# A third tile for the weighted values of a graph attention, in room taken from a buffer that is used only at the end

## The chip, the cores and the metric

The kernel runs on one core of a Trainium2 chip, as one launch. The metric is the device time of that core in microseconds (us), from the first instruction to the last. Six parts of the core appear below: PE (TensorE, the matrix multiplications, with PEld for its weight loads), DVE (VectorE), ACT (ScalarE), POOL (GpSimd, which here issues the gathers), SP (SyncE, which issues the other loads and stores), and the DMA engines that carry out the transfers.

## The reference

A layer of a graph network on 6250 nodes of 128 features and 200000 edges, which come sorted by their target node `dst`. Two convolutions over the edges come first, then the attention with 8 heads of 16 channels, which the change is about:

```
h = relu(layernorm(x))
h = mesh_conv(h, ...);  h = silu(group_norm(h)) + (silu(t_emb) @ tm_w + tm_b)
h = mesh_conv(h, ...);  h = silu(group_norm(h)) + h_in
q, k, v = (h @ qw + qb), (h @ kw + kb), (h @ vw + vb)      # n x 8 x 16 each
logits = (q[dst] * k[src]).sum(-1) * scale + (edge_attr @ ew + eb)
amax   = segment_max(logits, dst)
pe     = exp(logits - amax[dst])
ssum   = segment_sum(pe, dst)
w      = pe / clip(ssum[dst], 1e-06)
o      = segment_sum(w * v[src], dst)
out    = x + h + group_norm(o @ ow + ob)
```

All of it is in float32.

## The kernel before

The 200000 edges are cut into 196 chunks (`NCH`) of 1024 edges, that is 8 tiles (`TPC`) of 128 edges, one edge in each of the 128 partitions. The first convolution, the second and the attention each go through all chunks, one after the other; `pipeline` (L1011) writes the program of such a stage, and the class `Stage` of the attention gives it the steps. Each engine works through its instructions in the order in which the program issues them, and waits on semaphores for the others.

In step n of the attention the program issues, roughly in this order:

- `fetch` for chunk n + 2. SP loads the query table's rows (`pk`), the edges' relative targets (`rel`) and edge attributes; POOL issues eight indirect gathers (L314), each of which brings the key and value rows of 128 edges into one of eleven tiles `g`, `ge`, `gl`. The first gather of a chunk is held until PE's last product `qe` of an earlier chunk is through.
- `second` for a chunk s, which lies about a run of chunks behind: the one-hot `oh` of the edges' targets (L945 on DVE; for the last 40 chunks, `BY_ACT`, L1828 and L1829 on ACT), then `add_late`, which adds an earlier chunk's sums to the running sums (L1776, L1780, L1782 on DVE), then `sums` (L1757): 8 matmuls on PE, one for each tile (the trace counts each as two), of `oh` with the tile `v`, into one of two PSUM tiles `us0` and `us1` that take turns.
- `values_ahead` for the next chunk, s + 1: `weighted` (L1750 on DVE) writes the products of the gathered values with the weights `pe` into its tile `v`.
- `merge` for the chunk before, s - 1: L1790, L1793, L1764, L1766, L1767, L1768 on DVE compare its maxima, which `sums` left in `us`, with the running ones; L1770 and L1772 on ACT take two exponentials.
- `logits` for chunk n (L1687, L1692, L1695 on DVE, L1689 on ACT), `compared` (L940, L941 on ACT) and the products `qe` (L1672 on PE) for the next chunk.
- `early`: `columns` for the chunk after s + 1. ACT copies three groups of columns into that chunk's tile `v` (L1746, L1942, L1943).

The segment maxima are taken for runs of up to G = 8 chunks at once, by scans on DVE (L1722, L1725) between transposes on PE (L1718, L1729). The scans read segment marks, `nbs` and `nbe`, which `load_runs` (L1697) loads. The chunks are handled from the last edge to the first; `k.j` is NCH - 1 less the chunk's number, so it counts down to 0. Whenever a block of nodes has all its edges, its finishing (reciprocal of the sum L1266, output product L1105 and L1126, norm L1281 and below) is put between the steps.

The last seven steps (`ENDS`) follow an order written out by hand, the string `ENDING`; `ending` goes through its words, each a letter for the step and a number for the chunk's `j`. Its words n5, n3 and n1 load segment marks, in turn into the pool `bp` and into the pool `bq`.

A tile `v` holds 8 x 145 float32 values in each partition, 4640 bytes. It comes from a pool with two buffers:

```
k.v = vp.tile([P, TPC, VK + H + 1], FP, name="v", bufs=2)
```

so the columns of a chunk may be written once the sums of the chunk two before it have been read out. The pool `bq` is opened when the third chunk has been completed (`EARLY` = 3), at the point where the memory of a larger tile of the lead-in comes free:

```
if k.c == EARLY - 1:
    kept.ohs.close()
    gs[-1] = pool("gl", 1, side="right").tile([P, TPC, KV], FP, name="gl")
    self.bq = pool("bq", 1, side="right")
```

It holds one pair of marks, 2 x 2048 bytes in each partition. `lh_i` (L136) is a tile of indices of 784 bytes in each partition among the constants, and is used in the first convolution alone.

Of the kernel before, what the change touches and what calls it, by code (L numbers as in the profile page):

```python
# [11 lines left out]
FP = mybir.dt.float32  # L12
BF = mybir.dt.bfloat16
I32 = mybir.dt.int32
# [11 lines left out]
P = 128  # L26
D = 128
H = 8
# [3 lines left out]
TPC = 8  # L32
# [21 lines left out]
ENDS = 7  # L54
# [5 lines left out]
VK = H * (HD + 1)  # L60
# [7 lines left out]
def kernel(ctx: ExitStack, tc: tile.TileContext, x, src, dst, eat, w, out):  # L68
# [12 lines left out]
    NCH = -(-EI // TPC)  # L81
# [6 lines left out]
    const = ctx.enter_context(tc.tile_pool(name="const", bufs=1))  # L88
# [8 lines left out]
    hpc = gpc.enter_context(tc.tile_pool(name="hpc", bufs=1))  # L97
    kept = SimpleNamespace(h0=hpc.tile([P, NW, D], FP, name="h0"))
# [34 lines left out]
    nc.vector.tensor_scalar(minus_p, iota_p, -1.0, None, ALU.mult)  # L133
    src_i = const.tile([P, EW], I32, name="src_i")
    not_first = const.tile([P, 1], FP, name="not_first")
    lh_i = const.tile([P, NCH], I32, name="lh_i")  # L136
    wab = {}

    def new_wab(pool, i):
# [194 lines left out]
    def last_product():  # L334
        return next((i.name for i in reversed(nc.cur_bb.bb.instructions) if i.engine == mybir.EngineType.PE), None)
# [233 lines left out]
    def steps_of(i):  # L569


        ends, due, n = {}, {}, 0
        for m in spread(i):
            ends[n + m] = list(range(n, n + m))
            due.setdefault(n + m + (i == 3 or n < NCH - SOON), []).extend(ends[n + m])
            n += m
        waiting, todo, left = [], [], NCH
        while left:
            n = len(todo)
            waiting += due.get(n, ())  # L580
            steps = min([m for m in due if m > n], default=n + 1) - n
            k = -(-len(waiting) // steps)
            todo.append(waiting[:k])
            waiting = waiting[k:]
            left -= k
        return ends, todo
# [351 lines left out]
    def compared(k):  # L938

        nc.scalar.activation(k.ohT[:WN, :], k.rel, AF.Square, bias=minus_p[:WN])  # L940
        nc.scalar.activation(k.ohT[:WN, :], k.ohT[:WN, :], AF.Relu, bias=1.0, scale=-4.0)  # L941
# [686 lines left out]
    def attention(general=False):  # L1628
        if general:
# [3 lines left out]
        pool = lambda n, b, **kw: es.enter_context(  # L1633
            tc.tile_pool(name=f"{n}a{general:d}", bufs=b, reuse_waits="tile", **kw))
# [6 lines left out]
        gp, wk, vp = pool("gp", 1), pool("wk", 2), pool("vp", 1)  # L1641
# [13 lines left out]
        def banks():  # L1655
            return ps_.tile([P, 2, 512], FP, name="blk", tag="blk")
# [40 lines left out]
        def load_runs(run, bp):  # L1697

            nb = {}
            for name, d_ in (("nbs", nbs_d), ("nbe", nbe_d)):  # L1700
                nb[name] = bp.tile([G * H, EPC], BF, name=name)
                nc.sync.dma_start(
                    out=nb[name][:len(run) * H, :],
                    in_=d_[NCH - 1 - run[-1]:NCH - run[0], :, :].rearrange("c h e -> (c h) e"))
            return nb
# [35 lines left out]
        def heads(k):  # L1741
            return k.v[:, :, :VK].rearrange("p t (h c) -> p t h c", c=HD + 1)

        def columns(k):
            k.v = vp.tile([P, TPC, VK + H + 1], FP, name="v", bufs=2)
            nc.scalar.copy(heads(k)[:, :k.nt, :, HD], k.pe)  # L1746

        def weighted(k):
            v4 = heads(k)
            nc.vector.tensor_tensor(  # L1750
                v4[:, :k.nt, :, :HD], k.g[:, :k.nt, D:].rearrange("p t (h c) -> p t h c", c=HD),
                k.pe[:, :, :, None].to_broadcast([P, k.nt, H, HD]), ALU.mult)

        def sums(k, wide):
            k.u = us[k.c % 2]
            for t in range(k.nt):
                nc.tensor.matmul(k.u[:, :wide], lhsT=k.oh[:, t, :], rhs=k.v[:, t, :wide],  # L1757
                                 start=(t == 0), stop=(t == k.nt - 1))
# [38 lines left out]
        def add_late(k):  # L1797
            if k.j < ONE:
                add(k, t3[:, 0:1, :], 1)
            else:  # L1800
                add(k, t3[:, bass.ds(k.win, 2), :], 2)
# [21 lines left out]
        def halves_by_act(k):  # L1823
            k.oh = pools["oh"].tile([P, TPC, P], FP, name="oh")
            for t in range(k.nt):
                if t == TPC // 2:
                    yield
                nc.scalar.activation(k.oh[:, t, :], iota_j, AF.Square, bias=k.dm[:, t:t + 1], scale=-1.0)  # L1828
            nc.scalar.activation(k.oh[:, :k.nt, :], k.oh[:, :k.nt, :], AF.Relu, bias=1.0, scale=-1.0)  # L1829

        def onehot_by_pool(k, behind):
            k.oh = pools["oh"].tile([P, TPC, P], FP, name="oh")
            for t in range(k.nt):
                follows(nc.gpsimd.tensor_scalar(
                    k.oh[:, t, :], iota_j, k.dm[:, t:t + 1], None, ALU.is_equal), behind)

        class Stage:
# [3 lines left out]
            lg, j, both = None, 0, None  # L1841
# [14 lines left out]
            def complete(self, k):  # L1856

                for a in range(0, TPC, 4):
                    more = banks()
                    m4 = more.rearrange("p a (t c) -> p (a t) c", c=KV)  # L1860
                    for t in range(4):
                        nc.tensor.matmul(m4[:, t, :], lhsT=k.ohS[:, (a + t) * P:(a + t + 1) * P], rhs=late,
                                         start=True, stop=True)
                    nc.vector.tensor_tensor(k.g[:, a:a + 4, :], k.g[:, a:a + 4, :], m4, ALU.add)
                if k.c == EARLY - 1:
                    kept.ohs.close()
                    gs[-1] = pool("gl", 1, side="right").tile([P, TPC, KV], FP, name="gl")
                    self.bq = pool("bq", 1, side="right")

            def products(self, k):  # L1870
                products(k, [(k.ohT[:KW], k.pk[:KW])])
# [94 lines left out]
            def ending(self, ks, marks):  # L1966

                every = {NCH - 1 - c: k for c, k in ks.items()}
                every.update({k.j: k for k in self.sums + self.late})
                runs = {NCH - 1 - run[0]: [NCH - 1 - c for c in run] for run in steps_of(3)[0].values()}  # L1970
                of = {j: r for r, js in runs.items() for j in js}
                firsts, low, hot, lgs = {}, {}, {}, {}
                nbs = {of[ENDS - 1]: self.nb}
                seen = {ENDS - 3: last_product()}
                self.residuals_of_last()
                for word in ENDING.split():
                    what, j = word[0], int(word[1:])
                    k = every.get(j)
                    if what == "f":
                        kept.seen = seen[j]  # L1980
                        every[j] = self.fetch(NCH - 1 - j)
                        kept.seen = None
                    elif what == "c":
                        compared(k)
                    elif what == "q":
                        self.products(k)
                        seen[j - 2] = last_product()
                    elif what == "l":
                        firsts[j] = self.firsts(k)
                        next(firsts[j])  # L1990
                        lgs[of[j]] = self.lg
                    elif what in "ra":
                        next(firsts[j], None)
                    elif what == "n":
                        nbs[j] = load_runs([NCH - 1 - i for i in runs[j]], self.bp if len(nbs) % 2 == 0 else self.bq)
                    elif what == "t":
                        low[j] = maxima([every[i] for i in runs[j]], lgs[j], nbs[j], self.bp, True)
                        next(low[j])
                        next(low[j])
                    elif what in "szw":  # L2000
                        next(low[j], None)
                    elif what == "d":
                        self.columns(k)
                    elif what == "v":
                        weighted(k)
                    elif what == "o":
                        hot[j] = halves_by_act(k)
                        next(hot[j])
                    elif what == "p" and j in hot:
                        next(hot[j], None)  # L2010
                    elif what == "p":
                        onehot_by_pool(k, kept.behind)
                    elif what == "u":
                        sums(k, VK + H + 1)
                    elif what == "m":
                        self.merge(k)
                    else:
                        add_late(k)
                self.sum_residuals()
# [144 lines left out]
```

## Time and profile before

| | |
|---|---|
| time, median of 3 runs | 7012.45 us |
| the three runs | 7008.08, 7012.45, 7033.32 us |
| the profiled execution | 6977.15 us, with a span of 6975.4 us |
| PE busy in the span | 3884.5 us (56%) |
| DVE busy | 4886.9 us (70%) |
| ACT busy | 3365.8 us (48%) |
| POOL busy | 4465.4 us (64%) |
| DMA, mean rate over the span | 92 GB/s |

The span is the time between the first and the last instruction of the one execution that the profiler recorded. A row of the profile names the line, the engine, the operation and the tiles that it writes and reads, then the shapes. In the groups the time after the bar is the busy time of the group, then the mean of one instruction in ns, then how long the engine was idle just before these instructions, with what ended the idle time: "issue" is time in which the engine waited for nothing that the profile shows, "remote" an event that could not be put down to one instruction. In rows by time the first number is the start, in us from the start of the span, the second the length, and in brackets stands the idle time before it.

The attention takes the stretch from about 4690 us to the end of the span.

### The profile page before, as it was taken

What the parts mean: (1) busy time and instruction counts of PE and PEld (TensorE: products, weight loads), DVE (VectorE), ACT (ScalarE), POOL (GpSimd) and SP (SyncE); (2) the same over time, 40 slices, a digit from 0 to 9 for tenths busy, and PEclk for the clock granted to TensorE, in tenths of its full rate; (3) what the DMA queues carried; (4) which work ended last, traced back from release to release, by engine and by line L of the source; (5) the groups of instructions that cost most, each with busy time, mean ns of one, the idle gap of its engine ahead of it and who ended that gap; (6) DMA issues with size and microseconds to landing.
All of it is one profiled execution on the core that took longest, in us unless ns stands there. A gap on an engine that the chain in (4) does not pass through costs nothing. (4 is left out here: it accounts for less than half of the span.)

```text
span 6975.4 us, 66960 instructions
## 1 busy us (share of the span) xinstructions
PE 3884.5 (56%) x20796; PEld 3580.4 (51%) x20797; DVE 4886.9 (70%) x6981; ACT 3365.8 (48%) x5296; POOL 4465.4 (64%) x4714
## 2 busy tenths in 40 slices
PE   5555554555555555555555555545555565555555
PEld 4555554554455555555555454544455555445554
DVE  6677777776767667676777777755666667667766
ACT  5555555555555555555555555532222223223465
POOL 4666666666666666666666666665666666666664
PEclk8666666777777666666677777766776767767677
DMA  4223323322232222222233333333444444444442
GB/s 123 75 73 83 102 74 85 80 75 79 77 81 76 65 71 68 70 71 67 69 88 88 84 89 85 88 99 99 119 120 115 119 118 125 120 122 115 118 119 81
DMA packets 384808, 640.95 MB, mean 92 GB/s; under 512 B 91440, under 2 KB 250652, under 8 KB 382827
## 3 DMA queue, kind: packets, MB, share of 16 engines
q0 software_dynamic: 175056, 410.03, 22.4%
q1 hardware_dynamic: 208170, 226.05, 11.5%
q8 instruction: 168, 2.75, 0.2%
q14 instruction: 198, 1.62, 0.1%
q10 hardware_dynamic: 1216, 0.49, 0.0%
HBM read 588.85 MB, written 48.48 MB: 91 GB/s over the span
## 5 line engine op out<-in xcount | busy, mean ns | idle before, releaser
L314 POOL DMA_INDIRECT g<-b_d,src_i x3078 | 2917.0, 948 | 1590.5 <-issue 861.5
L1431 PE MATMUL u<-h,oh 128*128 128x129 f32 (+1 forms) x6252 | 1363.5, 393 | 1573.9 <-issue 963.0
L1431 PEld LDWEIGHTS u<-h,oh 128*128 128x128 f32 x6252 | 1231.0, 294 | 1706.6 <-issue 1056.4
L314 POOL DMA_INDIRECT g<-kv_d,src_i x995 | 948.0, 953 | 552.6 <-issue 270.0
L1392 PE MATMUL m<-pk,ohT 101*128 101x128 f32 x6252 | 1054.2, 327 | 331.3 <-issue 315.5
L1392 PEld LDWEIGHTS m<-pk,ohT 101*128 101x128 f32 x6252 | 991.5, 243 | 355.6 <-issue 340.6
L1757 PE MATMUL us<-v,oh 128*128 128x145 f32 x3126 | 670.0, 374 | 527.3 <-issue 242.7
L1399 DVE TENSOR_TENSOR h<-m,g 128x1024 f32<-128x1024 f32 x392 | 474.3, 1210 | 695.1 <-remote 640.9
L1757 PEld LDWEIGHTS us<-v,oh 128*128 128x128 f32 x3126 | 591.7, 260 | 602.0 <-issue 370.4
L1672 PE MATMUL qe<-pk,ohT 101*128 101x136 f32 x3126 | 566.3, 351 | 264.2 <-ACT ebs L1689 193.1
L1423 ACT ACTIVATE h<-h 128x1024 f32<-128x1024 f32 (+2 forms) x394 | 413.0, 1048 | 568.5 <-issue 414.1
L1672 PEld LDWEIGHTS qe<-pk,ohT 101*128 101x128 f32 x3126 | 526.2, 252 | 302.8 <-ACT ebs L1689 217.7
L940 ACT ACTIVATE ohT<-rel,minus_p 96x1024 f32<-96x1024 bf16 x588 | 668.9, 1138 | 15.6 <-issue 11.3
L941 ACT ACTIVATE ohT<-ohT 96x1024 f32<-96x1024 f32 x588 | 619.9, 1054 | 18.8
L1403 DVE TENSOR_REDUCE var<-sq 128x64 f32<-128x1024 f32 x392 | 474.2, 1210 | 172.1 <-ACT sq L1401 78.8
L314 POOL DMA_INDIRECT ge<-kv_d,src_i x408 | 388.9, 953 | 230.5 <-issue 109.7
L945 DVE TENSOR_TENSOR oh<-cps,dm 128x1024 f32<-128x1024 f32 x392 | 474.3, 1210 | 75.3 <-remote 65.8
L1436 ACT ACTIVATE u<-u,mask 128x129 f32<-128x129 f32 (+1 forms) x688 | 230.6, 335 | 533.5 <-remote 480.6
L1421 DVE TENSOR_TENSOR h<-h,cps 128x1024 f32<-128x1024 f32 (+2 forms) x394 | 477.4, 1212 | 13.5
L1422 DVE TENSOR_TENSOR h<-h,cps 128x1024 f32<-128x1024 f32 (+2 forms) x394 | 477.4, 1212 | 13.5
L1418 DVE TENSOR_TENSOR h<-h,cps 128x1024 f32<-128x1024 f32 (+2 forms) x394 | 474.5, 1204 | 0.8
L1401 ACT ACTIVATE sq<-h 128x1024 f32<-128x1024 f32 x392 | 411.6, 1050 | 119.8 <-DVE h L1399 101.5
(332 smaller groups left out, 4399.4 us busy)
## 6 DMA issues: line engine op xcount, KB each, us to landing
rel<-rel_d SPq DMA_DIRECT2D x291, 384.0 KB
g<-b_d,src_i POOLq DMA_INDIRECT x3078
pk<-a_d SPq DMA_DIRECT2D x552, 46.0 KB
g<-kv_d,src_i POOLq DMA_INDIRECT x995
ohT<-in_eat_dram SPq DMA_DIRECT2D x291, 40.0 KB
ge<-kv_d,src_i POOLq DMA_INDIRECT x408
a_d<-n_o SPq DMA_DIRECT2D x24, 256.0 KB
kv_d<-n_o SPq DMA_DIRECT2D x24, 256.0 KB
```

The costliest lines, as they stand in the source:

```text
L314: h = nc.gpsimd.indirect_dma_start(out=g[:, t, :table_d.shape[1]], out_offset=None, in_=table_d, in_offset=bass.IndirectOffsetOnAxis(ap=k. ...
L940: nc.scalar.activation(k.ohT[:WN, :], k.rel, AF.Square, bias=minus_p[:WN])
L941: nc.scalar.activation(k.ohT[:WN, :], k.ohT[:WN, :], AF.Relu, bias=1.0, scale=-4.0)
L945: return nc.vector.tensor_tensor(k.oh[:, :k.nt, :], iota[:, None, :].to_broadcast([P, k.nt, P]), k.dm[:, :, None].to_broadcast([P, k.nt, P ...
L1392: nc.tensor.matmul(k.m[:, t, :], lhsT=lhs[:, t * P:(t + 1) * P], rhs=rhs, start=(j == 0), stop=(j == len(terms) - 1))
L1399: nc.vector.tensor_tensor(k.mt, k.m[:, :n], k.g[:, :n], ALU.add)
L1418: nc.vector.tensor_tensor(m4, m4, k.rs.rearrange("p (t g) -> p t g", g=H)[:, a:a + n, :, None].to_broadcast([P, n, H, HD]), ALU.mult)
L1421: nc.vector.tensor_tensor(mt, mt, over_edges(gam, n), ALU.mult)
L1422: nc.vector.tensor_tensor(mt, mt, over_edges(bet, n), ALU.add)
L1431: nc.tensor.matmul(k.u[:, 0, :wide(k)], lhsT=k.oh[:, t, :], rhs=k.h[:, t, :wide(k)], start=start and t == 0, stop=stop and t == k.nt - 1)
L1672: nc.tensor.matmul(k.qe[:, t // TB, at:at + DB], lhsT=lhs[:, t * P:(t + 1) * P], rhs=rhs, start=(j == 0), stop=(j == len(terms) - 1))
L1757: nc.tensor.matmul(k.u[:, :wide], lhsT=k.oh[:, t, :], rhs=k.v[:, t, :wide], start=(t == 0), stop=(t == k.nt - 1))
```

## The change

The two buffers of the pool become two fixed tiles, v0 and v1, that are handed out in turn from a list. When the third chunk is complete, the memory that `bq` would take is given to a third tile, v2, which is put at the head of the list. From then on the three tiles take turns. Once a chunk's `j` is below ENDS + 4 = 11, v2 leaves the list; at the beginning of `ending` its pool is closed and `bq` is opened in its place. To make room for the 544 bytes by which v2 is larger than `bq`, `lh_i` moves from the constants to a pool (`hpc`) that is given up before the attention.

```diff
-    lh_i = const.tile([P, NCH], I32, name="lh_i")
+    lh_i = hpc.tile([P, NCH], I32, name="lh_i")
...
+        vs = [vp.tile([P, TPC, VK + H + 1], FP, name=f"v{j}") for j in range(2)]
+
         def columns(k):
-            k.v = vp.tile([P, TPC, VK + H + 1], FP, name="v", bufs=2)
+            if len(vs) > 2 and k.j < ENDS + 4:
+                vs[:] = [v for v in vs if v is not kept.third]
+            k.v = vs.pop(0)
+            vs.append(k.v)
             nc.scalar.copy(heads(k)[:, :k.nt, :, HD], k.pe)
...
                     gs[-1] = pool("gl", 1, side="right").tile([P, TPC, KV], FP, name="gl")
-                    self.bq = pool("bq", 1, side="right")
+                    self.more = ExitStack()
+                    more = self.more.enter_context(
+                        tc.tile_pool(name="v3a", bufs=1, side="right", reuse_waits="tile"))
+                    kept.third = more.tile([P, TPC, VK + H + 1], FP, name="v2")
+                    vs.insert(0, kept.third)
...
                 of = {j: r for r, js in runs.items() for j in js}
+                self.more.close()
+                self.bq = pool("bq", 1, side="right")
                 firsts, low, hot, lgs = {}, {}, {}, {}
```

The order of the instructions on each engine stays; what changes is where they wait. The first place is ACT, at the end of a step in the steady part of the attention (L1746 to L1943 are `columns`, L1770 and L1772 the exponentials of `merge`). Before, the copy into the tile v waited for PE:

```order
L1746 COPY v_23738<-pe_23573 128x8x8 [waits PE_49]
L1942 COPY v_23738<-wl_23571 128x8x8
L1943 ACTIVATE v_23738<-ef_118 128x8
L1770 ACTIVATE us1_22911<-d_23776 128x16 [waits DVE_49]
L1772 ACTIVATE be_23781<-d_23776 128x16 [waits DVE_49]
```

With the change the copy goes into one of the three fixed tiles:

```order
L1751 COPY v0_22919<-pe_23572 128x8x8
L1951 COPY v0_22919<-wl_23570 128x8x8
L1952 ACTIVATE v0_22919<-ef_118 128x8
L1775 ACTIVATE us1_22911<-d_23771 128x16 [waits DVE_49,PE_49]
L1777 ACTIVATE be_23776<-d_23771 128x16 [waits DVE_49]
```

The copy waits for nothing; the exponential, which writes into the PSUM tile of the sums, now carries the wait on PE. Of the 196 copies, 132 lose their wait on PE.

The second place is DVE in the same step: the end of `add_late`, `weighted`, and the start of `merge`. Before:

```order
L1782 TENSOR_TENSOR flat_94<-flat_94,us0_22910 128x272 [waits DVE_49]
L1750 TENSOR_TENSOR v_23738<-g7_22907,pe_23573 128x8x8x16 [waits Activation_49]
L1790 SCALAR_TENSOR_TENSOR nm_23770<-us1_22911,nm2_120 128x2
L1793 TENSOR_TENSOR cm_23772<-us1_22911,nm_23770 128x16 [waits DVE_49]
L1764 ISA
```

And with the change:

```order
L1787 TENSOR_TENSOR flat_94<-flat_94,us0_22910 128x272 [waits DVE_49]
L1755 TENSOR_TENSOR v0_22919<-g7_22907,pe_23572 128x8x8x16 [waits Activation_49]
L1795 SCALAR_TENSOR_TENSOR nm_23765<-us1_22911,nm2_120 128x2 [waits PE_49]
L1798 TENSOR_TENSOR cm_23767<-us1_22911,nm_23765 128x16 [waits DVE_49]
L1769 ISA
```

The merge's first instruction, which before needed no wait of its own since ACT's copy had waited for the same sums, now waits for PE itself. 128 of these instructions gain such a wait.

The third place is SP at the last seven steps, where the marks of word n5 go into the memory that v2 had. Before:

```order
L1702 DMA nbs<-nbs_d 16x1024 [waits DMAHW3_49]
L1702 DMA nbe<-nbe_d 16x1024 [waits DMAHW4_49]
L928 ISA
L928 DMA pk_854<-a_d_101 92x128 [waits DMAHW5_49,PE_49]
```

With the change the first of them waits for PE:

```order
L1702 DMA nbs<-nbs_d 16x1024 [waits DMAHW3_49,PE_49]
L1702 DMA nbe<-nbe_d 16x1024 [waits DMAHW4_49]
L928 ISA
L928 DMA pk_854<-a_d_101 92x128 [waits DMAHW5_49,PE_49]
```

## The prediction

> **What bounds the kernel now.** First the page, for the share of each engine:
>
> ```profile
> span 6975.4 us, 66960 instructions
> PE 3884.5 (56%) x20796; PEld 3580.4 (51%) x20797; DVE 4886.9 (70%) x6981; ACT 3365.8 (48%) x5296; POOL 4465.4 (64%) x4714
> ```
>
> No engine is near full, so the averages do not name the limit. The change touches the attention alone; the second view is the groups of instructions from 4690 to 6957 us (busy time, mean ns of one, then idle time just before it and what ended it):
>
> ```profile
> L314 POOL DMA_INDIRECT g<-kv_d,src_i x943 | 898.8, 953 | 526.9 <-issue 251.3 <-remote 120.0 <-DVE n_rec L1266 40.4
> L314 POOL DMA_INDIRECT ge<-kv_d,src_i x408 | 388.9, 953 | 230.5 <-issue 109.7 <-remote 39.7 <-PE qe L1672 23.2
> L314 POOL DMA_INDIRECT gl<-kv_d,src_i x136 | 129.3, 950 | 64.7 <-issue 35.9 <-remote 10.4 <-PE us L1757 5.8
> L1746 ACT COPY v<-pe 128x64 f32<-128x64 f32 x196 | 51.6, 263 | 446.4 <-remote 422.7 <-PE us L1757 14.6 <-PE qe L1672 4.6
> L1790 DVE SCALAR_TENSOR_TENSOR nm<-us,nm 128x2 f32<-128x2 f32 x172 | 25.5, 148 | 0.0
> ```
>
> Two things stand here. POOL's 943 + 408 + 136 = 1487 gathers (186 chunks of 8) hold it for 1417 us, and 822 us of idle time lie just before them: 2239 of the 2267 us. And ACT's copy into a v tile, L1746, stands 446 us, mostly for something remote, while the merge's first instruction, L1790, never stands. The view of waits from 4800 to 6800 us gives what this does to DVE:
>
> ```profile
> ACT v L1746 <- remote: 399.2, 37, 13.8
> DVE v L1750 <- ACT v L1746: 251.2, 43, 11.8
> POOL g L314 <- remote: 112.8, 43, 3.4
> DVE v L1750 <- issue: 88.5, 16, 11.2
> POOL g L314 <- DVE n_rec L1266: 40.4, 7, 8.1
> ```
>
> DVE stands 43 + 16 = 59 times before weighted (L1750), 339.7 us in all, about 5.8 us each. So there is a wait of the kind that a third tile can take away. Whether it counts is for POOL to say. Its row in time (start, length, what it does, idle time before):
>
> ```profile
> 5825.10 0.94 POOL L314 DMA_INDIRECT g<-kv_d,src_i  x1 [2.00 <-remote]
> 5826.34 0.95 POOL L314 DMA_INDIRECT g<-kv_d,src_i  x1 [0.30 <-issue]
> ...
> 5843.84 0.95 POOL L314 DMA_INDIRECT g<-kv_d,src_i  x1 [0.30 <-issue]
> 5848.18 0.95 POOL L314 DMA_INDIRECT g<-kv_d,src_i  x1 [3.39 <-PE us L1757]
> ...
> 5871.18 0.95 POOL L314 DMA_INDIRECT gl<-kv_d,src_i  x1 [2.59 <-remote]
> ```
>
> A gather starts every 1.25 us (0.95 + 0.30). After 16 of them comes a pause of about 3 us, and the runs start 23.08 and 23.00 us apart: 11.5 us for a chunk. Other runs have 8 gathers and a pause of about 2 us:
>
> ```profile
> 5909.59 0.94 POOL L314 DMA_INDIRECT ge<-kv_d,src_i  x1 [1.94 <-PE blk L1105]
> 5921.26 0.94 POOL L314 DMA_INDIRECT g<-kv_d,src_i  x1 [1.98 <-remote]
> ```
>
> That is 11.67 us for a chunk, nearly the same. 186 chunks at 11.5 to 11.67 are 2139 to 2171 us of the 2267. The rest, about 100 us, is the lead-in, a few longer pauses, and the work behind the last gather. So POOL's gathers set the pace of the attention.
>
> Last, what DVE, ACT and PE do in one of these runs:
>
> ```profile
> 5836.48 1.26 PE L1757 MATMUL us<-v,oh 128*128 128x145 f32 x8 [2.33 <-DVE us L1780]
> 5838.60 0.40 PE L1757 MATMUL us<-v,oh 128*128 128x145 f32 x1 [0.86 <-issue]
> ...
> 5846.37 0.84 PE L1757 MATMUL us<-v,oh 128*128 128x145 f32 x2 [1.01 <-issue]
> 5850.44 4.00 PE L1672 MATMUL qe<-pk,ohT 101*128 101x136 f32 x16 [3.23 <-ACT ebs L1689]
> ```
> ```profile
> 5846.39 0.27 ACT L1746 COPY v<-pe 128x64 f32<-128x64 f32 x1 [12.28 <-remote]
> 5850.11 0.28 ACT L1689 COPY ebs<-qe 128x48 f32<-128x48 f32 x2 [1.14 <-DVE g L1687]
> ```
> ```profile
> 5835.99 0.44 DVE L1782 TENSOR_TENSOR flat<-flat,us 128x272 f32 x1
> 5846.70 1.22 DVE L1750 TENSOR_TENSOR v<-g,pe 128x1024 f32<-128x1024 f32 x1 [10.28 <-issue]
> 5847.84 0.15 DVE L1790 SCALAR_TENSOR_TENSOR nm<-us,nm 128x2 f32<-128x2 f32 x1
> 5848.74 1.28 DVE L1687 TENSOR_TENSOR g<-qe,g 128x768 f32<-128x768 f32 x2
> 5854.15 1.21 DVE L1750 TENSOR_TENSOR v<-gl,pe 128x1024 f32<-128x1024 f32 x1
> ```
>
> PE starts the sums of a chunk at 5836.48, has eight of their 16 rows done in 1.26 us, and then single ones with gaps of 0.8 to 1.7 us until POOL's run is over. ACT's copy, which waits for the last of them since it wants that v tile, stands 12.28 us, and weighted behind it 10.28 us. From there DVE needs 7.45 us for a whole step (5846.70 to 5854.15), where POOL takes 11.5: DVE has 4 us to spare in each chunk, and the stall is where this spare time shows.
>
> **The change part by part.** *The third tile.* ACT's copy and weighted for a chunk no longer wait for the sums of the chunk two before it, but three before it, which are long done. In each of the 59 stalls ACT's copies (5846.39 to 5846.70, 0.31 us) and weighted (1.14 us to the start of L1790) move ahead of the wait: 1.45 us. But the very next thing that DVE does is L1790, which reads the sums of the same chunk that the copy waited for. In the new order it carries the wait on PE. So the wait goes from L1750 to L1790 and keeps all but 1.45 us of its length: of 339.7 us, 339.7 - 59 x 1.45 = 254 us stay. Queued behind L1790 on DVE are the merge, L1687 and the logits, as before; ACT's exps wait for DVE there anyway. Each stall ends as before, with DVE 1.45 us further on; summed over 59 that is 86 us of DVE time, the upper bound of what this part can give.
>
> What of it reaches the end? Behind the stall L1687, ebs and PE's next products at 5850.44 come 1.45 us earlier. POOL needs those products for the second half of its run, at 5858.18 (5848.18 + 8 x 1.25), and they are done at 5854.44 already: 3.7 us of cover becomes 5.2. Nothing is gained, as POOL does not stand there. At the run's end POOL restarts when PE's backlog is through, and PE's matmuls are in the same order with the same inputs: weighted for these sums was done a step before. I take 0 of the 86 us in the steady part.
>
> *The longer pauses.* Some are well over the usual 2 to 3.4 us:
>
> ```profile
> 5897.64 1.25 POOL L314 DMA_INDIRECT ge<-kv_d,src_i  x1 [6.47 <-DVE n_rec L1266]
> 5993.95 1.26 POOL L314 DMA_INDIRECT g<-kv_d,src_i  x1 [6.56 <-DVE n_rec L1266]
> ...
> 6785.69 0.95 POOL L314 DMA_INDIRECT g<-kv_d,src_i  x1 [7.98 <-PE blk L1105]
> 6837.83 0.94 POOL L314 DMA_INDIRECT ge<-kv_d,src_i  x1 [7.48 <-PE qe L1672]
> 6913.83 0.94 POOL L314 DMA_INDIRECT g<-kv_d,src_i  x1 [9.62 <-DVE blk L1722]
> ```
>
> Here POOL waits for the others, and 1.45 us of DVE's can count. The first kind occurs 7 times for g tiles, with 40.4 us; near the end there are a few. Of some ten such places I take three at 1.45 us: 4.5 us of gain. One more stall just ahead of the last chunks may reach the end: 1.5 us. Together 6 us, between 0 and 86.
>
> *The waits that move.* SP's load of the segment marks for the fifth of the last words now waits for PE to be done with the third tile. The load behind it on SP, pk, waits in both versions for a later product of PE, so nothing is held that was not held before: 0. If that cover were gone, the marks would come one chunk later, 11.5 us, once. ACT's one-hots in the last 40 chunks stand behind its v copies, and can now go before the sums are done; POOL's pace covers that too.
>
> *The addresses.* The 784 bytes of lh_i leave the constants, so all the tiles behind them lie lower. The three kinds of gather tile lie differently already, and cost 953, 953 and 950 ns: 0 for the gathers. For the other operations the bound is the largest difference between these rows, 3 ns: 4 us over 1487, either way.
>
> *The overlap.* Weighted ran at 5846.70, in POOL's pause, and will run in the middle of a run of gathers. One that already does so, at 5854.15, has this gather beside it, as long as any other, and the 1.25 us between starts is kept:
>
> ```profile
> 5854.43 0.95 POOL L314 DMA_INDIRECT g<-kv_d,src_i  x1 [0.30 <-issue]
> 5855.68 0.95 POOL L314 DMA_INDIRECT g<-kv_d,src_i  x1 [0.30 <-issue]
> ```
>
> So I take 0 for it. The Trainium skill, "SBUF — State Buffer", section "Who interferes with whom", speaks against the change here: a VectorE instruction with two inputs in SBUF contends with a GpSimd instruction that reads SBUF, and the loser blocks for the other's whole length; by it the sum would be 72 us worse (59 x 1.22, an estimate). The two rows do not agree with it.
>
> Sum: -6 us. The profiled run is 6977.15 us (its span and 1.75 us around it), so it would become 6971. The three timed runs have a median of 7012.45, 35 us above it, and the forecast is made there: 7012.45 - 6 = 7006.
>
> **The rivals.** *DVE's chain decides after all* (faster). If POOL's restart hangs on how far DVE is, and PE's slow matmuls shift with it, then up to 86 us go: 7012 - 86 = 6926. A smaller form: runs of 8 become runs of 16, since the products come 1.45 us earlier; at (11.67 - 11.5) x 186 that is at most 32 us, and with all ten long pauses shortened by 1.45 another 15: 6965. For it speaks that POOL's pauses end on remote and PE events; against it, that runs restart 23.0 us apart whether DVE had stood 10.28 us or 6.95 us:
>
> ```profile
> 5871.10 1.22 DVE L1750 TENSOR_TENSOR v<-ge,pe 128x1024 f32<-128x1024 f32 x1 [6.95 <-ACT v L1746]
> ```
>
> *The runs fall out of step* (slower). Every eighth chunk or so the finishing of a block of nodes (n_rec, L1266) is put on DVE, and where it meets a run's end POOL's pause is 6.5 us in place of about 3. By the waits this hits 7 of the some 23 blocks (186 chunks by 8) in g tiles. With DVE further on by 1.45 us the two meet elsewhere; if it hit ten blocks more, at 3.4 us each, the cost would be 34 us: 7046. If it hit all the 16 left, 54 us: 7066. It decides from ten blocks on. Against it: the shift is small against a run of 23 us.
>
> *Gathers slowed by the overlap* (slower): each moved weighted holds a gather for its own length, 59 x 1.22 = 72 us: 7084; against it stands the row of 0.95 us above. This is the case of the Trainium skill's rule on the shared ports.
>
> *The change does nothing at all*: the wait moves whole, and the time stays 7012; it can't be told from my forecast.
>
> **How the numbers follow.** I give the forecast 0.47 and the last case 0.08; DVE's chain 0.24, of which about 0.05 is its small form's part that stays within the bound; the runs out of step 0.18, of which 0.03 within; slowed gathers 0.03. What a measurement of this kernel can tell from no change is about 0.5%, 35 us: faster than 6977 or slower than 7048. That makes faster 0.19, slower 0.18, same 0.63; since the three timed runs alone span 25 us, and small shifts of phase over 186 chunks add up in a way the trace can't price, I move 0.06 from same to faster and 0.04 to slower: 0.25, 0.53, 0.22. The forecast's own range is 6985 to 7028. The range for 8 in 10 takes in half of each rival: 6935 to 7062.
>
> **What would show it.** In the new profile, ACT's v copy should stand almost nowhere for remote events, and DVE should stand at the merge's nm about 59 times for some 254 us (right), or much less (then the sums themselves came earlier, and the forecast is wrong). POOL's runs should still start 23.0 and 11.7 us apart, with pauses of 2 and 3.4 us and gathers of 0.95 us. Runs of 24 gathers, pauses under 1.5 us or products that start a run without pause would show DVE's chain as the limit; more pauses of 6.5 us would show runs out of step; gathers of over 1 us beside weighted would show the overlap's price. A shift of the time in the two convolutions would show that the addresses matter after all.

## The result and the profile after

The kernel with the third tile takes 7034.9 us (median of 14 runs, 7027.0 to 7044.06), the kernel before 7027.47 us in the same comparison (14 runs, 7008.08 to 7043.73). The ratio is 1.0013, with a 95% interval from 1.0005 to 1.0021: the change makes the kernel slower, by about 9 us (the two medians lie 7.4 us apart; the ratio here and in the tables below is the comparison's own estimate, not the quotient of the medians).

First, the wait moved as forecast. The long lines for ACT's copy into v and for weighted are gone from the view of waits of the changed kernel from 4800 to 6800 us, and there is a new one for the merge:

```profile
DVE nm L1795 <- remote: 307.7, 39, 10.6
...
POOL g L314 <- remote: 71.4, 26, 3.6
...
POOL g L314 <- DVE n_rec L1266: 41.0, 6, 7.0
...
POOL ge L314 <- DVE n_rec L1266: 13.3, 2, 6.8
```

And the groups of instructions of the attention show where the idle time went (busy time, mean ns, idle time before):

```profile
L1751 ACT COPY v<-pe 128x64 f32<-128x64 f32 x196 | 50.2, 256 | 8.2 <-remote 3.0 <-PE us L1762 1.8 <-DVE v L1755 1.4
...
L1795 DVE SCALAR_TENSOR_TENSOR nm<-us,nm 128x2 f32<-128x2 f32 x172 | 25.9, 150 | 316.7 <-remote 316.7
```

ACT's copy has 8 us of idle time left of 446, and the merge's first instruction has gone from none to 317 us. The last two lines of the waits matter more than they look: eight pauses of POOL of about 6.8 us, 54.3 us in all, that end with `n_rec`.

The profiled execution has a span of 7026.6 us, 51 us more than the one shown of before. Most of that is not the change: the kernel before, profiled once more, took 7030.9 us. The views of the gathers' line give the first and last start of each kind; `g<-b_e` belongs to the beginning of the second convolution, `g<-kv_d` to the attention. The changed kernel:

```profile
L314 POOL DMA_INDIRECT g<-kv_d,src_i x995: 940/946/1462, 4661.4 to 6979.2; - x199
...
L314 POOL DMA_INDIRECT g<-b_e,src_i x24: 938/944/947, 2352.0 to 2384.6; - x24
```

The kernel before in that second profile (the first experiment, e1):

```profile
L314 POOL DMA_INDIRECT g<-kv_d,src_i x995: 940/946/1436, 4667.5 to 6983.5; - x199
...
L314 POOL DMA_INDIRECT g<-b_e,src_i x24: 938/944/947, 2353.7 to 2386.1; - x24
```

Before the attention the two are within 6 us, and the gathers take the same 946 ns. The first profile came from an execution with shorter pauses everywhere. From here on profiles are compared by parts of the attention, and with others of the same pace.

For that, chunks are counted by POOL's gathers within the attention: count 104 is the moment at which 104 chunks have been gathered there. (Three more are gathered ahead of it, so the chunk that starts at count 104 is number 107 of the program.) A part's length is the time between the starts of two gathers. Five profiles of the same pace, in us:

| part, by count | before again (e1) | lh_i moved (e2) | lh_i moved, aligned (e4) | the change | the change, aligned (e3) |
|---|---|---|---|---|---|
| 0 to 22 | 282.4 | 286.8 | 283.0 | 280.8 | 281.2 |
| 22 to 86, eight groups of 8 chunks | 746.3 | 746.6 | 746.7 | 744.0 | 745.0 |
| 86 to 94 | 95.4 | 95.3 | 95.2 | 95.1 | 95.2 |
| 94 to 150, seven groups | 665.8 | 656.8 | 665.8 | 679.7 | 676.3 |
| 150 to the last full chunk, 191 | 511.9 | 512.5 | 509.3 | 503.9 | 510.8 |
| sum | 2301.7 | 2298.0 | 2299.9 | 2303.5 | 2308.5 |

With two tiles the means are 284.1, 746.5, 95.3, 662.8 and 511.2, with three 281.0, 744.5, 95.1, 678.0 and 507.3. So in the means the third tile gains 3.1 + 2.0 + 3.9 = 9 us in three parts, and loses 15.2 us in the groups from 94 to 150. The gains of the first and the last part are no larger than what two profiles of the same number of tiles differ by (up to 4.4 and 6.9 us); the loss is clear of that. These groups are where a block of nodes is finished every eight chunks. One such group takes about 94 us or 97 to 98 us, and nothing between: with two tiles 4 of 21 are long, with three tiles 13 of 14.

### The profile page after: what moved, and what is told of

The parts are those of the page before. It is cut to its first block, busy times and chain, and to the rows that moved or that the text cites. A ratio compares the mean times of both kernels' runs of the same rounds, so it can differ in the third digit from the quotient of the medians.

```text
span 7026.6 us, 67076 instructions
## 1 busy us (share of the span) xinstructions
PE 3897.8 (55%) x20796; PEld 3593.7 (51%) x20797; DVE 4891.8 (70%) x6981; ACT 3356.3 (48%) x5296; POOL 4462.4 (64%) x4714
## 5 line engine op out<-in xcount | busy, mean ns | idle before, releaser
L1775 ACT ACTIVATE us<-d 128x16 f32<-128x16 f32 x172 | 32.1, 187 | 1058.4 <-DVE d L1772 392.3
```

## Why a group takes 97 us

The row of POOL from count 104 on, in the changed kernel:

```profile
5901.94 0.95 POOL L314 DMA_INDIRECT g<-kv_d,src_i  x1 [3.48 <-DVE cm L1798]
...
5911.95 0.95 POOL L314 DMA_INDIRECT g<-kv_d,src_i  x1 [0.30 <-issue]
...
5925.23 0.94 POOL L314 DMA_INDIRECT gl<-kv_d,src_i  x1 [2.88 <-remote]
...
5951.87 1.25 POOL L314 DMA_INDIRECT ge<-kv_d,src_i  x1 [6.82 <-DVE n_rec L1266]
```

And with two tiles, at the addresses of the change (e2):

```profile
5912.93 0.96 POOL L314 DMA_INDIRECT g<-kv_d,src_i  x1 [3.47 <-PE us L1757]
...
5924.64 0.94 POOL L314 DMA_INDIRECT g<-kv_d,src_i  x1 [1.97 <-remote]
...
5948.08 0.95 POOL L314 DMA_INDIRECT ge<-kv_d,src_i  x1 [3.23 <-remote]
...
5959.94 1.08 POOL L314 DMA_INDIRECT ge<-kv_d,src_i  x1 [2.13 <-PE qe L1672]
```

With three tiles POOL goes on at count 105 (5911.95, no pause), takes 16 gathers, then 16 more, and meets count 108 at the end of a run of 16, with a pause of 6.82 us. With two it stops at 105 for 1.97 us, does a run of 16 to count 107, stops for 3.23, does 8, and stops at 108 for 2.13 us. These pauses are 9.7 us in the one case and 7.3 us in the other, and over the seven groups of the two profiles the difference of a whole group comes to 3.3 us (97.1 against 93.8).

Why it goes on at 105 shows in the products that POOL waits for. PE and DVE of the changed kernel:

```profile
5904.18 3.99 PE L1672 MATMUL qe<-pk,ohT 101*128 101x136 f32 x16 [1.80 <-ACT ebs L1689]
```
```profile
5901.55 0.16 DVE L1795 SCALAR_TENSOR_TENSOR nm<-us,nm 128x2 f32<-128x2 f32 x1 [10.31 <-remote]
...
5902.48 1.29 DVE L1687 TENSOR_TENSOR g<-qe,g 128x768 f32<-128x768 f32 x2
...
5909.98 1.28 DVE L1687 TENSOR_TENSOR g<-qe,g 128x768 f32<-128x768 f32 x2
```

And with two tiles (e2):

```profile
5915.88 3.99 PE L1672 MATMUL qe<-pk,ohT 101*128 101x136 f32 x16 [2.96 <-ACT ebs L1689]
```
```profile
5912.15 1.22 DVE L1750 TENSOR_TENSOR v<-g,pe 128x1024 f32<-128x1024 f32 x1 [11.09 <-ACT v L1746]
...
5914.18 1.28 DVE L1687 TENSOR_TENSOR g<-qe,g 128x768 f32<-128x768 f32 x2
...
5924.40 1.29 DVE L1687 TENSOR_TENSOR g<-qe,g 128x768 f32<-128x768 f32 x2 [2.68 <-remote]
```

With three tiles the products start 2.24 us after the run (5904.18 - 5901.94) and DVE uses them at 5909.98 without standing. With two they start 2.95 us after it (5915.88 - 5912.93) and end 6.94 us after it, and yet DVE, which wants them too, stands until 5924.40, when the run's gathers are over. The semaphore events in the traces, by which one engine tells the others of its progress, agree: PE's event for these products stands at 5909.08 in the changed kernel and only at 5924.38 in e2. This is PE's alone. In the changed kernel's runs of 8 gathers from count 22 to 150, none of PE's 85 events lies between 8 and 11 us after the run's start, where 67 of DVE's 367 lie. Whether PE's last work is late or only its event is not shown, as the ends of matmuls in a profile are modelled.

So PE's word that it is done comes in time when the products start up to some 2.4 us into a run of gathers, and mostly at the run's end when they start later. Ten profiles with eight such places each (counts 96, 104, ..., 152) show it: the first one of before, e1 to e4, the change, and e12, e15, e16 and e17 below.

| products start after the run's start | places | POOL goes on to 16 gathers | pause of 6 us or more three chunks later |
|---|---|---|---|
| up to 2.4 us | 36 | 36 | 35 (the other 5.95 us) |
| 2.5 to 2.6 us | 5 | 3 | 3 |
| 2.9 us or more | 39 | 2 | 2 |

With three tiles the place is at 2.23 us seven times of eight, both in the change and in e3; with two it is at 3.65 us in 13 of the 24 places of e1, e2 and e4. The difference of 1.42 us is close to the 1.45 us of ACT's copies and weighted. So it is the gain itself that would put the products on the other side of the limit; the experiments below try this.

What comes three chunks later is a wait that cannot be passed: the tile of the next gather was last read by a weighted whose weights hang on the maxima of the whole run of eight chunks. DVE of the changed kernel there:

```profile
5948.21 0.69 DVE L1733 TENSOR_TENSOR lg<-lg,blk 128x512 f32<-128x512 f32 x1 [2.54 <-remote]
...
5949.88 1.22 DVE L1755 TENSOR_TENSOR v<-ge,pe 128x1024 f32<-128x1024 f32 x1 [0.37 <-ACT v L1751]
```
```profile
5942.16 1.08 PE L1729 MATMUL blk<-ident,fw 64*128 64x64 f32 x8 [7.26 <-issue]
```

PE's last transposes for these maxima started at 5942.16, 16.9 us into the run, with 1.08 us of work. Their end, too, is seen only at 5948.21, after POOL's last gather of the run ended at 5945.06. From there L1733, L1736, the exponentials, the copies and weighted have to be done, until 5951.1, and POOL goes on at 5951.87. (The row of POOL names n_rec, which runs just behind weighted; by the semaphore events weighted ends at 5951.11 and POOL's wait for DVE at 5951.13.) With a pause one chunk earlier (count 107) the same transposes come 4.6 us after the start of the run of 8 at 5948.08, and DVE goes on without standing (e2):

```profile
5952.69 1.08 PE L1729 MATMUL blk<-ident,fw 64*128 64x64 f32 x8 [3.17 <-DVE nm L1790]
```
```profile
5956.12 0.68 DVE L1733 TENSOR_TENSOR lg<-lg,blk 128x512 f32<-128x512 f32 x1
```

Weighted is done at 5959.0, and POOL goes on at 5959.94, after the 2.13 us shown above.

## The experiments

**Is it the addresses?** Theory A says that the addresses cost, since everything behind `lh_i` moved by 800 bytes (its 784, padded), theory B that the third tile's own waits cost. (Theory C, that runs fall out of step, was formed from the profiles of these four.) e1 is the kernel before, unchanged. e2 moves the index tile alone:

```diff
-    lh_i = const.tile([P, NCH], I32, name="lh_i")
+    lh_i = hpc.tile([P, NCH], I32, name="lh_i")
```

e3 is the whole change, and e4 is e2, each with 32 bytes left free, so that the gather tiles lie at the same place within 256 bytes as before:

```diff
+    room = const.tile([P, 8], I32, name="room")
```

> The kernel before, unchanged, as a floor: every theory expects 0.999 to 1.001. Its profile says whether the shorter pauses of the first profile (16 gathers every 22.95 to 23.04 us in all three stages, span 6975 us) belong to that one execution, or to the program: the theory of the addresses expects 22.95 to 23.05 us again, the theory of an odd execution 23.15 to 23.25 us and a span near 7025 us.

> The index tile lh_i moved, two tiles v as before. Theory A (the addresses cost: gather tiles at 32 in place of 64 bytes past a multiple of 256): the whole loss, 1.001 to 1.003, in all three stages. Theory B (the third tile costs in the attention, since the wait at the merge's nm holds more than the one at the copy did): 0.999 to 1.0005.

> The change, with 32 bytes left free behind the constants, so that the gather tiles lie at the same place in a line of 256 bytes as before. Theory A (addresses): at or below the kernel before, 0.997 to 1.000. Theory B (third tile): as the change, 1.0005 to 1.002, with the loss in the attention alone.

> lh_i moved, 32 bytes left free, two tiles v: nothing of the change but a shift of 768 bytes. Theories A and B both expect 0.999 to 1.001; over 1.001 would say that the place counts in another way than by 64 bytes.

| | median us | ratio to before (7039.72 us) | 95% interval |
|---|---|---|---|
| e1, before again | 7037.56 | 0.9999 | 0.9989 to 1.001 |
| e2, lh_i moved | 7032.48 | 0.9998 | 0.9989 to 1.0006 |
| e3, change, aligned | 7044.36 | 1.0009 | 1.0 to 1.0018 |
| e4, lh_i moved, aligned | 7042.26 | 1.0004 | 0.9995 to 1.0013 |

Theory A falls: the addresses of the change with two tiles cost nothing (e2), and the change at the old alignment is still on the slow side (e3), though its interval touches 1. e1 also shows that the first profile was odd in its pace: in the steady groups 16 gathers came every 23.27 us, in the first profile every 23.03. The parts of these four profiles stand in the table above.

**Putting DVE back, in the wrong place.** If the gain of 1.45 us is what puts the runs out of step, then work that takes it back should make the kernel faster. e5 adds a reduction to the change that nobody reads:

```diff
+                if k.c % 8 == 6 and 94 <= k.c <= 150:
+                    spare = wk.tile([P, TPC, H], FP, name="l3")
+                    nc.vector.tensor_reduce(
+                        spare, k.g[:, :, D:].rearrange("p t (h c) -> p t h c", c=HD), AX.X, ALU.add)
                 yield from logits(k, self.lg[:, k.t0:, self.j, :])
```

e8 does the same to the kernel before; e6 takes the third tile out of the list at chunk 92, e7 puts it in at chunk 92:

```diff
-            if len(vs) > 2 and k.j < ENDS + 4:
+            if len(vs) > 2 and k.c >= 92:
```

> The change, with one more DVE instruction (a reduction over 128x1024 values, 1.2 us, whose result nobody reads) ahead of the logits of chunks 94, 102, ..., 150: it puts DVE back by about the 1.45 us that the third tile gained it, at the one place in each group of eight chunks where the two versions part. Theory C (out of step: with the earlier products POOL skips the pause after chunk 105 and its like, and pays 6.8 us after chunk 108): the pauses of 6.5 to 7 us at the node blocks 100, 108, ..., 156 fall from 8 to at most 2, groups of eight chunks from 97 back to 94 us, the attention 15 to 20 us shorter than with the change, 0.997 to 0.9995 of before. Theory B (the third tile itself costs, by its waits): groups of 97 us stay, the added 9 x 1.2 us come on top or are hidden, 1.001 to 1.003.

> The third tile is used up to chunk 91 only. Theory C: the lead-in and the steady groups as with the change (281 us, 93.0 us), the groups from chunk 94 on as with two tiles (94 to 98 us, mixed), the attention 2308 to 2314 us, 0.998 to 1.0. Theory B: the loss is spread, so about half of it stays: 1.0005.

> The third tile is used from chunk 92 on only. Theory C: the whole loss and none of the gain: lead-in 283 us, steady groups 93.4 us, groups from 94 on 97 us each (6 or 7 of 7), the attention 2322 to 2328 us, 1.001 to 1.003. Theory B: about half of the loss: 1.0005.

> The kernel before, with the same added reductions. Theory C: its groups of 97 to 98 us, of which it has 0 to 6 of 7 by chance, are gone or rare: 0.9985 to 1.0. Theory B: nothing or the added work, 1.0 to 1.0015.

The four measured 0.9997 (0.9988 to 1.0006), 0.9998 (0.9989 to 1.0007), 0.9997 (0.9988 to 1.0006) and 1.0000 (0.9991 to 1.0009), and the kernel before took 5978.66 us. The profiled executions had hardly a pause on POOL; e8, a kernel with two tiles, shows it in the page's busy times:

```profile
span 5972.0 us, 66960 instructions
...
PE 3627.6 (61%) x20796; PEld 3436.3 (58%) x20797; DVE 4909.5 (82%) x6989; ACT 3359.6 (56%) x5296; POOL 4475.4 (75%) x4714
```

POOL is busy for 4475 us, about as long as before (4465.4 us), in 1000 us less: the steady groups of eight chunks took 80.2 us with two tiles and with three, close to 64 gathers at 1.25 us. Where there are no runs, no theory can show, and no tile helps. e9, e10 and e11 put the same question again (e5, e7 and e8 once more):

> The change with the added reductions of 1.2 us once more, since the last four kernels met a chip on which POOL's gathers follow each other without a pause (before: 5978.66 us), so that there was no run to fall out of step. On a chip with the pauses, theory C (out of step): pauses of 6.5 to 7 us after chunks 100, 108, ..., 156 fall from 8 to at most 2, groups of eight chunks from 97 to 94 us, the attention 2299 to 2306 us, 0.997 to 0.9995 of before. Theory B (the third tile costs by its own waits): groups of 97 us stay, 1.001 to 1.003. On a chip without the pauses both expect 1.000.

> The third tile from chunk 92 on only, once more. On a chip with the pauses, theory C: lead-in 283 us and steady groups 93.4 us as with two tiles, then 6 or 7 of 7 groups at 97 us, the attention 2322 to 2328 us, 1.001 to 1.003. Theory B: about half of the change's loss, 1.0005.

> The kernel before with the added reductions, once more. On a chip with the pauses, theory C: groups of 97 to 98 us, of which two tiles have 0 to 6 of 7 by chance, are rare (at most 1): 0.9985 to 1.0. Theory B: 1.0 to 1.0015.

They ran without pauses too: 1.0003 (0.9994 to 1.0012), 1.0000 (0.9991 to 1.0009) and 1.0001 (0.9992 to 1.001) at 5965.01 us. e12, e5 a third time, had the pauses:

> The change with the added reductions of 1.2 us, a third time, for a chip on which POOL pauses after its runs of gathers. There theory C (out of step) expects groups of eight chunks back from 97 to 94 us from chunk 94 on, pauses of 6.5 to 7 us after chunks 100, 108, ..., 156 in at most 2 of 8 places, and 0.997 to 0.9995 of before; theory B (the third tile costs by its own waits) expects groups of 97 us and 1.001 to 1.003. On a chip without the pauses both expect 1.000.

It measured 1.0005 (0.9996 to 1.0014) at 6970.5 us. That missed what theory C expected: all groups from 94 to 150 stayed long, 96.1 to 96.4 us. The profile has the reason. The reduction of chunk 102 runs at 5815.63, and the logits that decide, behind the stall of the merge, are at 5849.63, three chunks later; in between stands the merge's wait, which can swallow the 1.2 us. The products that decide start 1.47 to 2.52 us after the run's start, no later than with the change. My count of the chunks had left out the three that are gathered ahead of the attention. So e12 says nothing against theory C, and serves as the change itself at the pace of 6970 us. It also says that the loss isn't shown at that pace: the groups from 94 to 150 take 674.0 us in e12 and 674.1 us in the first profile of before, the only one of the unaltered kernel at that pace, where seven of eight places went on to 16 gathers.

**Putting DVE back, in the right place.** e13 and e15 add two reductions to the change ahead of the logits of chunks 97, 105, ..., 153; e14 and e17 add them to the kernel before, and e16 adds four to the change:

```diff
+                if k.c % 8 == 1 and 97 <= k.c <= 153:
+                    for cols in (slice(0, D), slice(D, 2 * D)):
+                        spare = wk.tile([P, TPC, H], FP, name="l3")
+                        nc.vector.tensor_reduce(
+                            spare, k.g[:, :, cols].rearrange("p t (h c) -> p t h c", c=HD), AX.X, ALU.add)
                 yield from logits(k, self.lg[:, k.t0:, self.j, :])
```

> The change, with two added reductions (2.4 us of DVE, results unread) ahead of the logits of chunks 97, 105, ..., 153: the earlier ones stood ahead of chunks 94, 102, ..., three chunks before the place where a run of 16 gathers begins that decides, and changed nothing there. On a chip with pauses, theory C (out of step): the products behind these logits start 3.5 to 5 us after the run's start in place of 1.5 to 2.3, come too late for POOL to go on, the run ends after 8 gathers, the pauses of 6.5 to 7 us at the node blocks fall from 8 to at most 2, groups of eight chunks from 97 (chip of 7030 us) or 96.3 (chip of 6970 us) to 94 or 93; 0.997 to 0.9995 of before. Theory B (the third tile costs by its waits): the groups stay or grow by 2.4 us, 1.0005 to 1.003. On a chip without pauses both expect 1.000.

> The kernel before with the same two added reductions. On a chip with pauses, theory C: no group of over 95 us from chunk 94 to 150 (two tiles have 0 to 6 of 7 by chance): 0.9975 to 1.0. Theory B: 1.0 to 1.002. On a chip without pauses 1.000.

These two, e13 and e14, ran without pauses: 0.9996 (0.9987 to 1.0005) and 1.0000 (0.9991 to 1.0009), before 5968.77 us.

> The change with the two added reductions (2.4 us) ahead of the logits of chunks 97, 105, ..., 153, again, for a chip on which POOL pauses. Theory C (out of step): groups of eight chunks from chunk 94 to 150 back from 97 to 94 us (from 96.3 to 93 us on a chip whose steady groups take 92.4), pauses of 6.5 to 7 us at the node blocks in at most 2 of 8 places, 0.997 to 0.9995 of before. Theory B (the third tile's own waits): groups as with the change or 2.4 us longer, 1.0005 to 1.003. On a chip without pauses both expect 1.000.

> The change with four added reductions (4.8 us) ahead of the logits of chunks 97, 105, ..., 153. With two of them three of eight places still had their products at 1.5 to 2.4 us after the run's start and a pause of 6.5 us three chunks later. On a chip with pauses, theory C (out of step) expects products at 3.9 us or later in all eight places, no pause of over 6 us there, the seven groups from 94 to 150 at 93 to 94 us on average, and 0.9955 to 0.9985 of before. If the added work itself comes to count, the groups grow past 95 us and the ratio is over 0.999. Theory B (the third tile's own waits): 1.001 to 1.004. On a chip without pauses: 1.000 to 1.002.

> The kernel before with two added reductions (2.4 us) at the same places, on the same chip. On a chip with pauses, theory C: what was gained with three tiles (0.9976) came from the places in step, so two tiles get most of it: 0.9965 to 0.9990, with at most one pause of over 6 us from chunk 100 to 156, and a lead-in and steady groups as before. If the third tile is needed for the gain: 0.9995 to 1.001. On a chip without pauses 1.000.

| | median us | before, us | ratio | 95% interval | groups 94 to 150, us | pauses of 6 us or more, of 8 |
|---|---|---|---|---|---|---|
| e12, change, work misplaced | 6974.89 | 6970.5 | 1.0005 | 0.9996 to 1.0014 | 674.0 | 8 |
| e15, change, 2.4 us added | 6955.48 | 6974.19 | 0.9976 | 0.9967 to 0.9984 | 660.8 | 3 |
| e16, change, 4.8 us added | 6947.71 | 6967.97 | 0.9968 | 0.9958 to 0.9978 | 654.4 | 1 |
| e17, before, 2.4 us added | 6953.79 | 6967.97 | 0.9980 | 0.9969 to 0.9990 | 654.4 | 1 |

Work that nobody reads makes the changed kernel faster, where it puts the products past the limit. POOL's row of e16 from count 104 on, against that of the change above, has the pauses at 105, 107 and 108 back:

```profile
5844.60 0.95 POOL L314 DMA_INDIRECT g<-kv_d,src_i  x1 [3.38 <-DVE cm L1798]
...
5856.32 0.95 POOL L314 DMA_INDIRECT g<-kv_d,src_i  x1 [2.01 <-PE qe L1672]
...
5879.43 0.94 POOL L314 DMA_INDIRECT ge<-kv_d,src_i  x1 [3.19 <-remote]
...
5891.12 1.26 POOL L314 DMA_INDIRECT ge<-kv_d,src_i  x1 [1.97 <-DVE n_rec L1266]
```

DVE and PE of the same stretch show the added work and the products behind it, 6.73 us after the run's start (5851.33 - 5844.60):

```profile
5845.13 4.59 DVE L1894 TENSOR_REDUCE l<-g 128x64 f32<-128x1024 f32 x4
5849.64 1.28 DVE L1687 TENSOR_TENSOR g<-qe,g 128x768 f32<-128x768 f32 x2
```
```profile
5851.33 3.99 PE L1672 MATMUL qe<-pk,ohT 101*128 101x136 f32 x16 [6.07 <-issue]
```

Theory B, by which the added work should have come on top, falls with e15 and e16. Theory C holds, with two misses in its numbers: in e15 three places, not at most two, kept the long pause (with 2.4 us added, their products still started at 1.47, 1.66 and 2.37 us); and in e16 one place, at count 128, went on although its products started at 4.61 us. So the limit is not one number for all places. In the groups from 94 to 150, e15 gains 13.2 us on e12 and e16 gains 19.6 us.

e17 answers the other question: two tiles get most of the gain too. It is the gain of the runs in step: the groups from 94 to 150 take 654.4 us in both. On top of it e16 is 6.1 us faster than e17 by the medians, in the same comparison. The other parts of its profile are 3.6 us shorter in sum, nearly all of it after count 150 (503.8 against 507.1), and the steady groups are 1.0 us longer; and the two intervals overlap. So what the third tile itself is worth isn't settled. At the pace with pauses e16 has the lowest median of all, and e15, e16 and e17 are faster than the kernel before, by 0.2 to 0.3%. All three ran at the pace of 6970 us; at that of 7030 us, where the loss of the change was measured, the added work was not tried, and there the account rests on the rows above.

## Why the prediction was wrong

The forecast was 6 us of gain, and 9 us of loss were measured. The time lay well within the wide range, 6935 to 7062 us; the direction was wrong. By its steps:

- **The wait moves to the merge and keeps its length but for 1.45 us.** Right for the long waits, and too large in the sum. Of the waits of over 5 us the median went from 10.36 us (e1, at weighted) to 8.91 us (the change, at the merge), which is 1.45 us. But 307.7 us are left in the view of waits against the 254 us forecast. Only 39 waits are left, since many were too short to give 1.45 us: in e1 22 of 58. Before weighted e1, e2 and e4 have 330, 315 and 326 us of waits, and at the merge the change and e3 have 308 and 300: DVE got about 20 us in all, not 86.
- **POOL's gathers set the pace, and keep 1.25 us.** Right, and by this the upper bound of 86 us was out of reach. The 253 gathers that run beside a weighted in the changed kernel take 946 ns on average, the 222 in e1 945 ns, so the overlap cost nothing.
- **The gain of 6 us.** Perhaps right in kind, and not settled: lead-in, steady groups and end gave 3.1 + 2.0 + 3.9 = 9 us in the means, with a spread between profiles as large. The long pauses, where 4.5 of the 6 us were to come from, did get shorter at the node blocks (7.5 to 7.8 us in e1, e2 and e4, 6.5 to 7.0 us with the change), but there were eight of them in place of one to three.
- **"Nothing is gained, as POOL does not stand there."** This is the step that failed. It took the end of PE's products (5854.44) as the moment from which POOL can go on, and so found 3.7 us of cover. What counts is when that end is seen during a run of gathers, and the limit lies near a start of 2.4 to 2.9 us after the run's start. POOL does stand there, for about 2 us, where the products come later than that (1.97 us in e2), and whether it does sets the pause three chunks on. The products that I had quoted started at 2.26 us (5850.44 - 5848.18), already on the near side; at other places of the same kernel they start at 3.65 us, and those are the ones that a shift of 1.45 us takes across.
- **The runs fall out of step.** This rival was the right mechanism: the block of nodes, the pause of 6.5 us, 3.4 us for each (measured: 3.3 us for a group). I gave it 0.18 because the shift was small against a run of 23 us. That was the wrong yardstick; it had to be held against the distance to the limit, 1.2 us. And the count was off: with ten blocks more it would have cost 34 us, but only the eight places from 96 to 152 were hit, of which one to three were hit already with two tiles in the profiles at this pace. So 15 us were lost, and what the other parts gained took back some of it. In the first profile of before seven of the eight places were out of step already, which hid that most need not be.
- **Addresses and SP's wait at nothing.** Right for the addresses, by e2. SP's wait was not tried alone.

Why two tiles fall on either side from one execution to the next (one, two, three and seven of eight places go on to 16 gathers) is open; so is what holds PE's word back while POOL gathers.

## What to carry to other kernels

When two engines run in a rhythm, a gain on an engine with time to spare is not simply lost: it can move an event across a limit, and the pattern that follows may be dearer. So look at the spread over all repetitions for how far each release lies from the point where it decides, not at one of them, and price a shift by that distance. A quick test is to add idle work at the suspected place: if the kernel gets faster, the order of events was the cost, and not the work.

## What was not expected of the hardware

The kernel before had medians of 5965 to 5979 us in three comparisons and 6968 to 7040 us in the others, with gathers of 0.95 us in both. In the faster case POOL issues a gather every 1.25 us without a stop; in the other the runs of 8 and 16 mostly end with a pause of about 2.0 or 3.3 to 3.6 us, and of the products that started 2.9 us or more into a run, the ends were seen only after it in 37 places of 39. The granted clock of the profiled executions was 0.751 to 0.759 in the faster case and 0.698 to 0.707 in the other. No run shows what makes the difference. It does not go with the number of the chip: e9 to e11 (without pauses) and e16 and e17 (with them) are on record with the same one, 11. A change like this one can be judged only where the pauses are: without them the third tile in a part of the chunks, the added work, and both together all measured 0.9996 to 1.0003.
